# A graph layer over 1.65 million edges: 16 rows per block fetched one by one by SP and ACT beside POOL's gathers

## The chip, the core and the metric

The kernel runs on one core of one Trainium2 chip. The engines named here are PE (TensorE, matrix products), PEld (its weight loads), DVE (VectorE), ACT (ScalarE), POOL (GpSimd) and SP (SyncE, which issues transfers). The metric is the device time of one launch in microseconds (us). Before the change it was 15710.4 us, the median of three runs from 15699.01 to 15711.42 us.

## The reference

One layer of a graph network on 50000 nodes with 128 features each, followed by a residual and a normalization of each row. Every edge has a source node, a destination node and a type, 0 or 1, and the type chooses which of two weight matrices makes the message. The edges are sorted by destination.

```python
Xs = X[src]
m_data = Xs @ W_data.T + b_data
m_ctrl = Xs @ W_control.T + b_control
msg = jnp.where((edge_types == 0)[:, None], m_data, m_ctrl)
agg = jax.ops.segment_sum(msg, dst, num_segments=X.shape[0])
out = jax.nn.relu(agg + (X @ W_self.T + b_self))
x = _layernorm(x + out, axis=-1)
```

There are 1,650,000 edges: 800,000 random ones in both directions, and one loop from each node to itself.

## The kernel before, in words

The kernel doesn't compute a message per edge. It first sums the rows `x[src]` of all edges with the same destination and type, and multiplies these sums by the two weight matrices afterwards. The number of edges per destination and type is counted too, since each adds one bias.

The sorted edge list is cut into blocks. A block (`b`) has two steps (`Q = 2`), and a step has twelve chunks (`R = 12`) of 128 edges. For each chunk POOL issues one indirect DMA (L428, in `gathers`), which fetches 128 rows of 512 bytes, one to each partition. A pass is six chunks into one tile `y`; there are ten such tiles (`SLOTS = 10`), so POOL may be 60 gathers ahead of PE. A semaphore per tile says when the rows have landed, and PE waits for it at L435. Each step covers a window of 60 destinations (`W = 60`), and for each chunk PE multiplies the rows by a one-hot matrix `oh` (128 edges by 60 destinations by two types) into the sum `acc` of the step (L447). Two more small products add the counts (L451).

Loops from a node to itself need no fetched row, because the block's own rows of `x` are loaded anyway. Their places in the chunks are filled with other edges, up to `F = 42` per step (`fill`), so that a step takes 1536 + 42 edges from the list. The first block and the last one are plain: no places are filled there, and the last takes what is left over. With 3156 edges in a full block there are 523 blocks, 53 groups of ten, and the last block has 21 gathers.

DVE does most of the other work. Per block and in this order, it adds the last step's sum of the block before into a ring of three tiles (`add`, L458), begins the next tile (`begin_sums`, L471), makes the one-hot matrix two blocks ahead (`onehot`, L403) and its counts (`counts`, L411), fills the lists five blocks ahead (`fill`, L304 to L326, with an integer shift at L318), adds the first step's sum (L458), takes moments of the block before (L487 to L494) and makes a matrix `z` of the places that were filled (`left_out_matrix`, L341), which PE and then DVE (L358) use. Every second block it normalizes two blocks of rows (`store`, L509 and L512), after a square root on ACT (L503). Once in ten blocks it prepares the lists of the next group (`columns`, L212 to L282). Some of its operands are copied to PSUM first, `num_ps` and `lists` for instance.

PE's `layer(b - 1)` (L477 to L481) multiplies the sums by the weights; it stands in PE's order in block `b`, after the first two passes. SP loads the block's own rows three blocks ahead (`window`, L397), the edge lists of a group (`load_edges`, L159 and L161), the filling lists (L289 and L294) and stores the result (L517). ACT has only the square root to do in the steady state.

The order of the work is written out by hand (`tc.manual_schedule()`): each engine takes its instructions in the order of the program, and the loop over blocks at the end of `straight` sets that order. Semaphores between engines are placed by the framework, save those of the gathers.

Of the kernel before, what the change touches and what calls it, by code (L numbers as in the profile page):

```python
# [2 lines left out]

# [20 lines left out]
D = 128  # L24
ROW = 4 * D
# [8 lines left out]
R = 12  # L34
W = 60
Q = 2
PASS = 6
B = 112
C = R * Q
F = 42  # L40
R1 = R + 1
C1 = Q * R1
SIZES = [P] * R
SIZE = sum(SIZES)
CE = Q * SIZE
BE = CE + Q * F
NBLK = 2 + (E - CE) // BE
REST = E - CE - (NBLK - 2) * BE
REST_ROWS = [min(n, max(0, REST - q * SIZE - sum(SIZES[:r]))) for q in range(Q) for r, n in enumerate(SIZES)]
# [2 lines left out]
GB = 10  # L52
GROUPS = -(-NBLK // GB)
GC = GB * C1
AHEAD = 2
# [17 lines left out]
TBL = GROUPS * GB  # L73
# [4 lines left out]
def plain(b):  # L78

    return b == 0 or b >= NBLK - 1  # L80
# [3 lines left out]
    return bass.AP(tensor=ap.tensor, offset=ap.offset, ap=[[0, n], *ap.ap])  # L84


def straight(ctx, tc, c, x, x_t, edges_t, edges_f, dst_first, first_p, out):

# [12 lines left out]
    nc = tc.nc  # L101
# [3 lines left out]
    eds = ctx.enter_context(tc.tile_pool(name="eds", bufs=2))  # L105
# [48 lines left out]
    nc.vector.memset(stats, 0.0)  # L154
    loops = keep.tile([P, GROUPS], F32, name="loops")

    def load_edges(g):
# [219 lines left out]


    idxs = {0: idx0}
    bys, pcs, zs, pls, bases = {}, {}, {}, {}, {}  # L380
    ohs, cnts, accs, xTs, pos, hs, mvs, sds, os_ = {}, {}, {}, {}, {}, {}, {}, {}, {}

    BASES = 4
# [23 lines left out]
    def counts(b):  # L407

        cnt = ohp.tile([P, Q, 2 * W], BF16, name="cnt")
        with nc.allow_low_precision(reason="whole numbers up to R1"):  # L410
            nc.vector.tensor_reduce(cnt, ohs[b].rearrange("p (q r) w -> p q w r", r=R1), AX.X, ALU.add)  # L411
        cnts[b] = cnt

    landed = [tc.alloc_semaphore(f"landed{i}") for i in range(SLOTS)]
    seen = [0] * SLOTS
    pass_no = [0]
# [20 lines left out]
    def products(b, q, ks):  # L439
        y = gathers(b, ks)  # L440
        of_step = chunks_of(b, q)
        if ks[0] == of_step[0]:
            accs[b, q] = ps.tile([P, 3, W], F32, name="acc")
        acc = accs[b, q]
        for k in ks:
            r = REST_ROWS[k] if b == NBLK - 1 else SIZES[k % R]
            nc.tensor.matmul(acc[:, :2, :].rearrange("p t w -> p (t w)"), y[:r, k % PASS, :], ohs[b][:r, column(k), :],  # L447
                             start=k == of_step[0], stop=k == of_step[-1])
        if ks[-1] == of_step[-1]:
            for t in range(2):  # L450
                nc.tensor.matmul(acc[:, 2, :], to_row[:, t, :], cnts[b][:, q, t * W:(t + 1) * W],  # L451
                                 start=t == 0, stop=t == 1)
# [44 lines left out]
    def pair(b):  # L497

        return range(b // 2 * 2, b + 1) if b % 2 == 1 or b == NBLK - 1 else ()
# [19 lines left out]
    def find_bad():  # L519
# [35 lines left out]
    for b in range(1, RAHEAD):  # L555
        fill(b)
        left_out_columns(b)
        left_out_matrix(b)
        if b < AHEAD:
            onehot(b)  # L560
            counts(b)
        if b == 1:
            clear_sums()
    for b in range(NBLK + 1):
        if b == NBLK - 1:
            find_bad()
        if b + 3 < NBLK:
            window(b + 3)
        g, i = divmod(b, GB)
        if i == 0 and g + 1 < GROUPS:  # L570
            load_edges(g + 1)
        if i == 3 and g + 1 < GROUPS:
            spread_out(g + 1)
        if i == 4 and g + 1 < GROUPS:
            spread_in(g + 1)
        if b > 0:
            add(b - 1, steps_of(b - 1)[-1])
        if b < NBLK:
            begin_sums(b)
        if b + AHEAD < NBLK:  # L580
            onehot(b + AHEAD)
            counts(b + AHEAD)
        last = steps_of(b)[-1:]
        for q, (step, ks) in enumerate(passes_of(b)):
            if ks:
                products(b, step, ks)
            if q == 0 and b > 0:
                left_out_columns(b + RAHEAD - 1)
            if q == 0 and b + RAHEAD < NBLK:
                fill(b + RAHEAD)  # L590
            if q == 1 and b > 0:
                layer(b - 1)
            if q == 1:
                left_out_numbers(b + 1)
            if ks and step not in last and ks[-1] == chunks_of(b, step)[-1]:
                add(b, step)
            if q == 1 and b > 0:
                moments(b - 1)
# [235 lines left out]
@with_exitstack  # L834
def gnn_resnorm(
    ctx: ExitStack,
    tc: tile.TileContext,
    x: bass.AP,
    x_t: bass.AP,
    edges_t: bass.AP,  # L840
    edges_f: bass.AP,
    dst_first: bass.AP,
    first_p: bass.AP,
    src: bass.AP,
    dst: bass.AP,
    etype: bass.AP,
    w_data: bass.AP,
    b_data: bass.AP,
    w_ctrl: bass.AP,
    b_ctrl: bass.AP,  # L850
    w_self: bass.AP,
    b_self: bass.AP,
    out: bass.AP,
):

    nc = tc.nc  # L860
    const = ctx.enter_context(tc.tile_pool(name="const", bufs=1))

    ident = const.tile([P, P], F32, name="ident")
    make_identity(nc, ident)
    eps = const.tile([P, 1], F32, name="eps")
    nc.vector.memset(eps, EPS)
    wmsgT = const.tile([P, 2 * D], F32, name="wmsgT")
    wselfT = const.tile([P, D], F32, name="wselfT")
    w_all = const.tile([P, 3, D], F32, name="w_all")
    with tc.tile_pool(name="wts_ps", bufs=3, space=bass.MemoryType.PSUM) as wts_ps:  # L870
        for i, (w, o) in enumerate(((w_data, wmsgT[:, :D]), (w_ctrl, wmsgT[:, D:]), (w_self, wselfT))):
            w_sb = w_all[:, i, :]
            nc.scalar.dma_start(w_sb, w)
            pw = wts_ps.tile([P, D], F32, name="pw")
            nc.tensor.transpose(pw, w_sb, ident)
            nc.scalar.copy(o, pw)
    bad = const.tile([1, 1], I32, name="bad")
    c = dict(ident=ident, eps=eps, wmsgT=wmsgT, wselfT=wselfT, bad=bad,
             b_data=b_data, b_ctrl=b_ctrl, b_self=b_self)

    with ExitStack() as own:
        straight(own, tc, c, x, x_t, edges_t, edges_f, dst_first, first_p, out)
# [53 lines left out]
```

## Time and profile before

| what | value |
|---|---|
| median of the runs | 15710.4 us (15699.01 to 15711.42) |
| the profiled execution's own time | 15700.48 us |
| its span | 15698.7 us |
| granted TensorE clock | 0.53 of full speed |
| DMA packets | 563631, 935.70 MB, 60 GB/s |
| gathers by POOL | 12528 with lists from DVE and from the first load, 21 of the last block |

The profile is one execution of the program. Its page has the busy time of each engine, the span in 40 slices, the DMA queues, the chain of work that ended last, and groups of instructions. A group's line gives the line of the kernel, the engine, the operation, what it writes and reads with the shapes, its count, then its busy time in us and the mean ns of one, and then the idle time of the engine just ahead of these instructions with what ended it. "issue" is time in which an engine waited for nothing that the profile shows. Lines of the waits read: who waited, for what, in total us, how often, the longest. Lines of the timeline read: start in us, length in us, engine, line, operation, operands, count, and in brackets the idle time ahead with what ended it. PE's ends are modelled, and instructions follow one another in a pipeline, so the distance between starts tells more than lengths.

### The profile page before, as it was taken

What the parts mean: (1) busy time and instruction counts of PE and PEld (TensorE: products, weight loads), DVE (VectorE), ACT (ScalarE), POOL (GpSimd) and SP (SyncE); (2) the same over time, 40 slices, a digit from 0 to 9 for tenths busy, and PEclk for the clock granted to TensorE, in tenths of its full rate; (3) what the DMA queues carried; (4) which work ended last, traced back from release to release, by engine and by line L of the source; (5) the groups of instructions that cost most, each with busy time, mean ns of one, the idle gap of its engine ahead of it and who ended that gap; (6) DMA issues with size and microseconds to landing.
All of it is one profiled execution on the core that took longest, in us unless ns stands there. A gap on an engine that the chain in (4) does not pass through costs nothing. (4 is left out here: it accounts for less than half of the span.)

```text
span 15698.7 us, 108076 instructions
## 1 busy us (share of the span) xinstructions
PE 7588.4 (48%) x34677; PEld 6800.0 (43%) x34678; DVE 11054.2 (70%) x13586; ACT 80.8 (1%) x268; POOL 11852.3 (75%) x12559
## 2 busy tenths in 40 slices
PE   4444444444444444444444444444444444444444
PEld 3444444444444444444444444444444444444444
DVE  8766777777776776777777776677777777667775
ACT  0000000000000000000000000000000000000000
POOL 7777777777777777777777777777777777777777
PEclk6555555555555555555555555555555555555555
DMA  2222222222222222222222222222222222222222
GB/s 63 60 59 60 60 59 60 60 59 60 59 60 60 59 60 59 60 60 59 60 60 59 60 60 59 60 59 60 59 60 60 59 60 60 59 60 60 59 60 56
DMA packets 563631, 935.70 MB, mean 60 GB/s; under 512 B 289617, under 2 KB 348580, under 8 KB 563056
## 3 DMA queue, kind: packets, MB, share of 16 engines
q0 software_dynamic: 401600, 823.20, 20.2%
q1 hardware_dynamic: 161018, 105.30, 2.5%
q8 instruction: 281, 4.60, 0.1%
q14 instruction: 294, 2.41, 0.1%
q10 hardware_dynamic: 438, 0.20, 0.0%
HBM read 897.64 MB, written 30.17 MB: 59 GB/s over the span
## 5 line engine op out<-in xcount | busy, mean ns | idle before, releaser
L428 POOL DMA_INDIRECT y<-in_x,idx x12528 | 11830.7, 944 | 3824.1 <-issue 3568.3
L447 PE MATMUL acc<-oh,y 128*128 128x120 f32 x25098 | 6060.6, 431 | 7948.3 <-PEq L435 7948.3
L447 PEld LDWEIGHTS acc<-oh,y 128*128 128x128 f32 x25098 | 5478.4, 328 | 8434.5 <-PEq L435 8424.3
L458 DVE TENSOR_TENSOR sums<-acc,sums 128x180 f32 x1046 | 354.7, 339 | 4258.6 <-PE acc L451 4256.9
L411 DVE TENSOR_REDUCE cnt<-oh 128x240 bf16<-128x3120 f32 x523 | 3045.1, 5822 | 17.8
L403 DVE TENSOR_TENSOR oh<-col,small 128x3120 f32<-128x3120 f32 x523 | 1774.8, 3394 | 0.0
L326 DVE TENSOR_REDUCE by<-old 128x84 bf16<-128x1092 f32 x521 | 1108.0, 2127 | 18.1
L307 DVE TENSOR_TENSOR m<-rk,small 128x1092 f32<-128x1092 f32 x521 | 672.9, 1291 | 17.8
L310 DVE TENSOR_TENSOR new<-m,small 128x1092 f32<-128x1092 f32 x521 | 672.8, 1291 | 17.7
L314 DVE TENSOR_REDUCE v_new<-new 128x26 f32<-128x1092 f32 x521 | 672.5, 1291 | 17.7
L323 DVE TENSOR_TENSOR old<-m,small 128x1092 f32<-128x1092 f32 x521 | 668.8, 1284 | 0.0
L481 PE MATMUL po<-wmsgT,sums 128*112 128x128 f32 x2092 | 525.5, 394 | 0.0
L481 PEld LDWEIGHTS po<-wmsgT,sums 128*112 128x112 f32 x2092 | 381.6, 252 | 109.3 <-issue 87.5
L479 PE MATMUL po<-bias,sums 3*112 3x128 f32 x1046 | 355.6, 435 | 0.0
L451 PEld LDWEIGHTS <-to_row 128*128 128x128 bf16 x2092 | 328.7, 157 | 51.3
L471 DVE TENSOR_TENSOR sums<-pl,sums 128x336 f32<-128x336 f32 x521 | 264.4, 507 | 82.0 <-DVE sums L458 44.5
L451 PE MATMUL acc<-cnt,to_row 128*128 128x60 bf16 x2092 | 321.0, 247 | 0.0
L478 PE MATMUL po<-wselfT,xT 128*112 128x128 f32 x1046 | 319.9, 408 | 0.0
L478 PEld LDWEIGHTS po<-wselfT,xT 128*112 128x112 f32 x1046 | 281.7, 318 | 0.0
L479 PEld LDWEIGHTS po<-bias,sums 3*112 3x112 f32 x1046 | 209.6, 254 | 122.6 <-issue 113.9
L477 PE MATMUL po<-ident,xT 128*112 128x128 f32 x523 | 230.5, 441 | 0.0
L341 DVE TENSOR_SCALAR z<-node_no,at 84x256 bf16<-84x256 f32 x521 | 204.2, 392 | 18.4
(115 smaller groups left out, 3184.3 us busy)
## 6 DMA issues: line engine op xcount, KB each, us to landing
y<-in_x,idx POOLq DMA_INDIRECT x12528, 2.5
xT<-in_x_t SPq DMA_DIRECT2D x523, 56.0 KB, 1.9
out<-o SPq DMA_DIRECT2D x523, 56.0 KB, 1.6
vf_all<-vd SPq DMA_DIRECT2D x53, 420.0 KB, 3.6
sdt<-in_edges_t SPq DMA_DIRECT2D x53, 390.0 KB
sdt_f<-in_edges_f SPq DMA_DIRECT2D x53, 9.8 KB
vd<-v_f SPq DMA_DIRECT2D x53, 3.3 KB
first_i<-in_dst_first SPq DMA_DIRECT2D x1, 530.0 KB
```

Source lines behind the costliest of these rows:

```text
L307: nc.vector.tensor_tensor(m, rk_g[g][:, i, :, None].to_broadcast([P, C1, F]), rank_no_ps[:, None, :].to_broadcast([P, C1, F]), op=ALU.is_e ...
L310: nc.vector.tensor_tensor(new.rearrange("p (q r) f -> p q r f", r=R1), m.rearrange("p (q r) f -> p q r f", r=R1), vf.rearrange("p (q f) -> ...
L314: nc.vector.tensor_reduce(v, new, AX.X, ALU.add)
L323: nc.vector.tensor_tensor(old, m, cb[:, :, None].to_broadcast([P, C1, F]), op=ALU.mult)
L326: nc.vector.tensor_reduce(by, old.rearrange("p (q r) f -> p q f r", r=R1), AX.X, ALU.add)
L403: nc.vector.tensor_tensor(oh, col_g[g][:, i, :, None].to_broadcast([P, C1, 2 * W]), num_ps[:, None, :].to_broadcast([P, C1, 2 * W]), op=AL ...
L411: nc.vector.tensor_reduce(cnt, ohs[b].rearrange("p (q r) w -> p q w r", r=R1), AX.X, ALU.add)
L428: copy = nc.gpsimd.indirect_dma_start(out=y[:r, k % PASS, :].bitcast(U8), out_offset=None, in_=x_rows, in_offset=bass.IndirectOffsetOnAxis ...
L447: nc.tensor.matmul(acc[:, :2, :].rearrange("p t w -> p (t w)"), y[:r, k % PASS, :], ohs[b][:r, column(k), :], start=k == of_step[0], stop= ...
L451: nc.tensor.matmul(acc[:, 2, :], to_row[:, t, :], cnts[b][:, q, t * W:(t + 1) * W], start=t == 0, stop=t == 1)
L478: nc.tensor.matmul(po, xT, c["wselfT"], start=True, stop=False)
L481: nc.tensor.matmul(po, a[:, t, :B], c["wmsgT"][:, t * D:(t + 1) * D], start=False, stop=t == 1)
```

## The change

Each step takes eight more edges from the list, whose rows aren't gathered by POOL. SP and ACT fetch four of them each, with ordinary transfers of one row of 512 bytes. For that, the source numbers of these edges come in a list of their own (`src_x`), loaded on SP with the other lists of a group. DVE multiplies the 16 numbers of a block by the row size (`offsets`, three blocks ahead). SP and ACT each load eight of the results into registers with one instruction and issue eight transfers (`single_rows`, two blocks ahead, after the first pass of a block). PE waits for two semaphores once per block (`rows_fetched`) and adds one product with eight rows to each step's sum. The destination and type of these edges stand in the thirteenth column of the step's lists, which was there before and held no edges, so the one-hot matrix covers them without more work. A full block takes 3172 edges; there are 521 blocks, and the last one has 6 gathers.

```diff
+TURNS = (4, 4)
+S = sum(TURNS)
+LOADS = 1
+BEGIN = (0, -(-Q * TURNS[0] // 4) * 4)
+X = BEGIN[1] + -(-Q * TURNS[1] // 4) * 4
-BE = CE + Q * F
+BE = CE + Q * (F + S)
...
     def load_edges(g):
+        t = eds.tile([1, GB * X], I32, name="one_g")
+        nc.sync.dma_start(t, src_x[None, g * GB * X:(g + 1) * GB * X])
+        one_g[g] = t
...
+    ROW_SLOTS = AHEAD + 2
+    fetched = [[tc.alloc_semaphore(f"fetched{j}_{i}") for i in range(ROW_SLOTS)] for j in range(2)]
+
+    def offsets(b):
+        if not plain(b):
+            g, i = divmod(b, GB)
+            ats[b] = stp.tile([1, X], I32, name="at_x", bufs=AHEAD + 2)
+            nc.vector.tensor_scalar(ats[b], one_g[g][:, i * X:(i + 1) * X], float(ROW), None, op0=ALU.mult)
+
+    def single_rows(b, part):
+        if part == 0:
+            ys[b] = stp.tile([S, Q, D], F32, name="yx", bufs=ROW_SLOTS)
+        both = []
+        for j, (eng, dma) in enumerate(((SP, nc.sync), (ACT, nc.scalar))):
+            n = Q * TURNS[j]
+            k0, k1 = part_of(n, part), part_of(n, part + 1)
+            at = BEGIN[j]
+            _, rows = nc.values_load_multi_w_load_instructions(ats[b][0:1, at + k0:at + k1], engines=[eng], **RANGE)
+            both.append([(dma, fetched[j][b % ROW_SLOTS], *divmod(k0 + k, TURNS[j]), sum(TURNS[:j]), row)
+                         for k, row in enumerate(rows)])
+        for pair in zip_longest(*both):
+            for dma, sem, q, k, at, row in filter(None, pair):
+                copy = dma.dma_start(ys[b][at + k:at + k + 1, q, :].bitcast(U8), x_bytes[:, bass.ds(row, ROW)])
+                copy.then_inc(sem, 16)
...
+    def rows_fetched(b):
+        times = len(range(b % ROW_SLOTS or ROW_SLOTS, b + 1, ROW_SLOTS))
+        for j in range(2):
+            wait = nc.tensor.wait_ge(fetched[j][b % ROW_SLOTS], 16 * Q * TURNS[j] * times)
+        tc.declare_fence(wait.ins, group=f"single{b}")
...
         if ks[-1] == of_step[-1]:
+            if not plain(b):
+                if q == 0:
+                    rows_fetched(b)
+                nc.tensor.matmul(acc[:, :2, :].rearrange("p t w -> p (t w)"), ys[b][:, q, :],
+                                 ohs[b][:S, q * R1 + R, :], start=False, stop=True)
...
+    for b in range(1, AHEAD + 1):
+        offsets(b)
     columns(0)
...
             begin_sums(b)
+        offsets(b + AHEAD + 1)
         if b + AHEAD < NBLK:
             onehot(b + AHEAD)
...
+            if q < LOADS and not plain(b + AHEAD):
+                single_rows(b + AHEAD, q)
```

More of the change, by code (lines that the diff above doesn't have):

```diff
@@ L2 @@
 from contextlib import ExitStack
+from itertools import zip_longest
 import concourse.bacc as bacc
@@ L84, in row_bcast, with straight @@
     return bass.AP(tensor=ap.tensor, offset=ap.offset, ap=[[0, n], *ap.ap])
-def straight(ctx, tc, c, x, x_t, edges_t, edges_f, dst_first, first_p, out):
+def straight(ctx, tc, c, x, x_t, edges_t, edges_f, src_x, dst_first, first_p, out):
     nc = tc.nc
@@ L155, in straight @@
     loops = keep.tile([P, GROUPS], F32, name="loops")
+    one_g = {}
     def load_edges(g):
+        t = eds.tile([1, GB * X], I32, name="one_g")
+        nc.sync.dma_start(t, src_x[None, g * GB * X:(g + 1) * GB * X])
+        one_g[g] = t
         t = eds.tile([P, 3, GB, C1], I32, name="sdt", bufs=1)
@@ L379, in straight @@
     idxs = {0: idx0}
-    bys, pcs, zs, pls, bases = {}, {}, {}, {}, {}
+    bys, pcs, zs, pls, bases, ats, ys = {}, {}, {}, {}, {}, {}, {}
     ohs, cnts, accs, xTs, pos, hs, mvs, sds, os_ = {}, {}, {}, {}, {}, {}, {}, {}, {}
@@ L412, in counts, with part_of @@
         cnts[b] = cnt
+    ROW_SLOTS = AHEAD + 2
+    RANGE = dict(min_val=0, max_val=(N - 1) * ROW, skip_runtime_bounds_check_because="where a node's row is")
+    x_bytes = x.rearrange("n d -> (n d)").bitcast(U8)[None, :]
+    fetched = [[tc.alloc_semaphore(f"fetched{j}_{i}") for i in range(ROW_SLOTS)] for j in range(2)]
[4 more added lines that the diff above has]
+            nc.vector.tensor_scalar(ats[b], one_g[g][:, i * X:(i + 1) * X], float(ROW), None, op0=ALU.mult)
+    def part_of(n, part):
+        return min(n, 32 * part)
+    def single_rows(b, part):
[13 more added lines that the diff above has]
+                copy.then_inc(sem, 16)
+                tc.no_tile_sem_insts.add(copy.ins.name)
+                tc.add_to_no_dep_group(f"single{b}", copy.ins)
+    def rows_fetched(b):
[3 more added lines that the diff above has]
+        tc.declare_fence(wait.ins, group=f"single{b}")
     landed = [tc.alloc_semaphore(f"landed{i}") for i in range(SLOTS)]
@@ L447, in products @@
             nc.tensor.matmul(acc[:, :2, :].rearrange("p t w -> p (t w)"), y[:r, k % PASS, :], ohs[b][:r, column(k), :],
-                             start=k == of_step[0], stop=k == of_step[-1])
+                             start=k == of_step[0], stop=plain(b) and k == of_step[-1])
         if ks[-1] == of_step[-1]:
+            if not plain(b):
[3 more added lines that the diff above has]
+                                 ohs[b][:S, q * R1 + R, :], start=False, stop=True)
             for t in range(2):
@@ L561, in straight @@
             counts(b)
+            for part in range(LOADS):
+                single_rows(b, part)
         if b == 1:
@@ L841, in gnn_resnorm @@
     edges_f: bass.AP,
+    src_x: bass.AP,
     dst_first: bass.AP,
@@ L881, in gnn_resnorm @@
     with ExitStack() as own:
-        straight(own, tc, c, x, x_t, edges_t, edges_f, dst_first, first_p, out)
+        straight(own, tc, c, x, x_t, edges_t, edges_f, src_x, dst_first, first_p, out)
     found = nc.values_load(bad, min_val=0, max_val=4 * P,
@@ L904 @@
         rest = a[CE:].reshape(TBL - 1, BE)
-        steps = rest.reshape(TBL - 1, Q, SIZE + F)
+        steps = rest.reshape(TBL - 1, Q, SIZE + F + S)
         cols = np.full((TBL, Q, R1, P), pad, np.int32)
@@ L911 @@
             cols[NBLK - 1, :, r, :n] = rest[NBLK - 2, :CE].reshape(Q, SIZE)[:, at:at + n]
+        cols[1:NBLK - 1, :, R, :S] = steps[:NBLK - 2, :, SIZE + F:]
         fills = np.full((TBL, Q, F), pad, np.int32)
         fills[1:NBLK - 1] = steps[:NBLK - 2, :, SIZE:SIZE + F]
+        ones = np.full((TBL, X), pad, np.int32)
+        single = steps[:, :, SIZE + F:]
+        for j, n in enumerate(TURNS):
+            ones[1:, BEGIN[j]:BEGIN[j] + Q * n] = single[:, :, sum(TURNS[:j]):][:, :, :n].reshape(TBL - 1, Q * n)
         firsts = np.ascontiguousarray(cols[:, :, 0, 0])
@@ L916 @@
         fillers.append(fills.reshape(TBL * Q, F))
+        if k == "src":
+            arrays["src_x"] = ones.reshape(-1)
         if k == "dst":
@@ L929 @@
     with tile.TileContext(nc) as tc:
-        gnn_resnorm(tc, ap["x"], ap["x_t"], ap["edges_t"], ap["edges_f"], ap["dst_first"], ap["first_p"],
+        gnn_resnorm(tc, ap["x"], ap["x_t"], ap["edges_t"], ap["edges_f"], ap["src_x"], ap["dst_first"], ap["first_p"],
                     ap["src"], ap["dst"], ap["edge_type_2"],
```

## The prediction

> **What bounds the kernel now.** I read the page's busy table first, then its groups, then the waits of POOL, then the timeline of one block and of the end.
>
> ```profile
> span 15698.7 us, 108076 instructions
> PE 7588.4 (48%) x34677; PEld 6800.0 (43%) x34678; DVE 11054.2 (70%) x13586; ACT 80.8 (1%) x268; POOL 11852.3 (75%) x12559
> L428 POOL DMA_INDIRECT y<-in_x,idx x12528 | 11830.7, 944 | 3824.1 <-issue 3568.3
> L447 PE MATMUL acc<-oh,y 128*128 128x120 f32 x25098 | 6060.6, 431 | 7948.3 <-PEq L435 7948.3
> L458 DVE TENSOR_TENSOR sums<-acc,sums 128x180 f32 x1046 | 354.7, 339 | 4258.6 <-PE acc L451 4256.9
> ...
> POOL y L428 <- issue: 3574.7, 11728, 0.3
> POOL y L428 <- PE acc L447: 3.5, 2, 3.2
> POOL y L428 <- DVE idx L318: 2.1, 1, 2.1
> ```
>
> No engine is busy over 75%, yet one has no slack. A gather is 0.944 us of work and 0.305 us of POOL's own issue, and (11830.7 + 3824.1) / 12528 = 1.2496 us per gather accounts for nearly the whole span. Read gather by gather, the distance between starts is 1.244 to 1.260 us in 99 of 100. POOL waited for others only twice, both at the start; the idle times of 0.3 us that other lines put down to PE or DVE are the same issue time. PE and DVE sit idle waiting for rows: PE 7948 us for landed gathers, DVE 4257 us for PE's sums. So the time is the number of gathers times 1.2496 us, plus a start and an end. A block of 24 gathers lasts 30.0 us.
>
> **What goes.** A full block takes 2·(1536+42) = 3156 edges before, and 2·(1536+42+8) = 3172 after, with the same 24 gathers. Blocks: 2 + (1650000 − 3072)//3156 = 523, and 2 + 1646928//3172 = 521. Rest for the last block: 2652 edges in 21 gathers before, 660 in 6 after. Gathers: 522·24 + 21 = 12549 before, 520·24 + 6 = 12486 after. 63 fewer, by 1.2496 us: **−78.7 us**. All of it is on the path, if the pitch stays.
>
> **SP and ACT.** Each gets 519 blocks times one register load and 8 one-row transfers. The nearest rows are SP's window load (0.37 us to issue) and ACT's one-row bias loads (0.23 to 0.56 us): 8 × 0.37 + 0.3 = 3.3 us per queue in a 30 us block. They are issued in the order of block b, for block b+2, and PE needs them some 45 us later. On SP the next window load (three blocks ahead) and the stores queue behind them; on ACT a square root each second block, which only a normalization waits for. Cost 0 under this cover. Without it, a late row would stop PE, and POOL only after the 60 gathers (75 us) that its ten slots hold.
>
> **The DMA engines.** The gathers take 20.2% of them, all else 2.8%; 8304 transfers of 512 bytes add about 4 MB to 936. What they do to POOL's pitch the trace does not show directly. Nearest: gathers beside the 1046 window loads and stores stand within 1 ns of the others. Bounds −1 to +1 ns per transfer, ±8 us; I take 0.
>
> **PE.** One product more per step, two matmuls. In the block below, twelve loads run from 8014.52 to 8017.02, so a pair is 0.42 us; 1038 steps make 436 us beside 7948 us idle. Cost 0 for PE, but each step's sum is ready 0.42 us later.
>
> **DVE.** One small multiplication per block (L437 after: 1x16). Nearest rows: 0.14 us for 1x1 (L536), 0.18 us for 128x26 (L318); back to back such operations start 0.08 us apart. 519 × 0.08 = 42 us beside 4257 us idle: cost 0 for DVE's own time.
>
> **Where the two shifts matter.** DVE's chain of a block starts at the wait for the last step's sum and runs without another wait to z (L341). So z moves by 0.42 + 0.08 = 0.50 us against the gathers, whose beat stays. The timeline shows why that can cost:
>
> ```profile
> 8006.89 0.94 POOL L428 DMA_INDIRECT y<-in_x,idx  x1 [0.30 <-issue]
> 8007.54 0.41 DVE L341 TENSOR_SCALAR z<-node_no,at 84x256 bf16<-84x256 f32 x1
> 8008.14 0.94 POOL L428 DMA_INDIRECT y<-in_x,idx  x1 [0.30 <-issue]
> 8014.52 2.64 PEld L447 LDWEIGHTS acc<-oh,y 128*128 128x128 f32 x12 [4.87 <-PEq L435]
> 8017.02 0.36 PEld L451 LDWEIGHTS <-to_row 128*128 128x128 bf16 x2
> ...
> 11513.73 0.35 DVE L341 TENSOR_SCALAR z<-node_no,at 84x256 bf16<-84x256 f32 x1
> 11513.84 1.06 POOL L428 DMA_INDIRECT y<-in_x,idx  x1 [0.30 <-issue]
> ```
>
> Usually z starts 0.55 to 0.68 us after a gather and disturbs nothing (it is itself held, 0.41 for 0.35 us); in some 200 blocks at 0.92, because an integer shift ahead of it (L318) was held in the same way, which 0.5 us later it no longer is. In the last two lines DVE was late, z began 0.11 us ahead of a gather, and the gather took 1.06 for 0.94 us. Eight z of 521 did this: leads of 0.19, 0.15, 0.13 and 0.11 us cost 0.04, 0.07, 0.09 and 0.11 us, that is 0.22 minus the lead. Two that began 0.05 us after a gather's start cost nothing; between a lead of 0.10 and those there is no row. After the change z stands at 0.65 + 0.50 = 1.15 us, a lead of 0.10, with a spread of about ±0.06 from block to block. That is the edge. I take half the blocks at 0.10 us each: 519 × 0.05 = **+26 us**. Low end: all miss, 0. High end by the rows: all at 0.12 us, 62 us. The other ten-block work of DVE (L214, L267) prolongs some gathers today, about 8 us in all; it may vanish or double, ±8 us.
>
> A rule of the Trainium skill speaks against the change here ("SBUF — State Buffer", section "Who interferes with whom"): a tensor_scalar in a two-port mode and a GpSimd operation exclude each other for the whole instruction, whichever comes second waiting. By it each z and each new multiplication could hold a gather for its length, by an estimate from the rows 519 × (0.35 + 0.15) = 260 us, and the kernel would end near 15900 us. The rows above agree that either side can wait, but not that each overlap costs POOL.
>
> **Start and end.** The first index list and PE's first products hang on DVE's preparation (the waits of 2.1 and 3.2 us). One more load is issued on SP before first_i (0.4 us), and two multiplications come first: **+0.7 us**. At the end the last block has one pass instead of four, and the layer of the block before it no longer hides beside later gathers. PE's order puts it after the last rows, then DVE's moments and stores, and only then the last sum:
>
> ```profile
> 15686.95 0.44 PE L477 MATMUL po<-ident,xT 128*112 128x128 f32 x1
> 15687.17 0.35 DVE L458 TENSOR_TENSOR sums<-acc,sums 128x180 f32 x1 [6.48 <-PE acc L451]
> 15688.45 1.20 PE L481 MATMUL po<-wmsgT,sums 128*112 128x128 f32 x4
> 15689.68 0.29 DVE L487 COPY h<-po 112x128 f32<-112x128 f32 x1 [2.16 <-PE po L481]
> ```
>
> Added are a layer (15686.95 to 15689.65: 2.7 us), moments (1.2), root and reciprocal (0.5), two normalizations (0.6) and the add (0.5), less 0.3 to 0.5 us of the last layer that no longer waits: **+5 us** (3 to 6).
>
> **Sum.** −78.7 + 26 + 0.7 + 5 = −47 us, against the profiled execution's own 15700.5 us (span 15698.7 and 1.8 around it). That execution is 9.9 us below the median of the runs shown (15699.0 to 15711.4). On the median: 15710.4 − 47 = **15663 us**.
>
> **Rivals.**
> 1. z lands in front of every gather and each lead counts. Between leads of 0.10 and 0 there is no row; if the line 0.22 minus lead went on, 0.20 us per block would cost 104 us, and −78.7 + 5.7 + 104 = +31 us gives 15741 us, **slower** by 0.2%. It decides from 73/519 = 0.14 us per block on. For it: the line holds in all eight rows, and the shift points just there. Against it: two z 0.05 us after a start were harmless, and when z comes while POOL is using the port, z waits, as its 0.41 us show.
> 2. z misses every gather, because the shift is 0.60 rather than 0.50 us (a product more than 0.42 us, a multiplication waiting on its two queues). Then −73 us: 15637 us.
> 3. The one-row transfers drag on the gathers, or arrive late and stop PE. At 5 ns per gather the first costs 62 us: 15726 us. The 1 ns beside transfers of 56 KB speaks against it, and the 45 us of lead against the second; but ACT has issued no DMA in the steady state so far, so this is not seen.
> 4. The change does not do what it says: the count of gathers is fixed by the sizes and not by the chip, so only the pitch is open. I give this nothing.
>
> **How the numbers follow.** About 0.2% (31 us) is what can be told from no change. Forecast, collisions of 10 to 42 us: 0.50, at 15647 to 15679. Rival 2: 0.20, faster. Collisions of 42 to 104 us: 0.17, within 0.2%. Rival 1 beyond that: 0.08, slower. Rival 3: 0.05, of which 0.03 slower. Together faster 0.70, same 0.19, slower 0.11. The range runs from the case without collisions less the 12 us between runs, 15625, to collisions of 85 us, 15722; below lies about 0.04, above about 0.15. Cases of both signs are in it; the forecast's own range is 15640 to 15685.
>
> **What the profile after would show.** POOL's indirect group counts 12480 and 6. Its mean is 944 ns by rival 2, 946 by the forecast (26 us over 12486), 952 by rival 1, so single gathers beside z tell more. Right: z starts 0.0 to 0.2 us ahead of a gather, about half of those gathers at 1.04 to 1.06 us; idle per gather stays 0.305 us; no wait of PE on fetched rows; the last gather stands some 21 us before the end instead of 16.5. Wrong: a pitch that is longer in all gathers (rival 3), gathers of 1.1 us and more in each block (rival 1), or a POOL wait named after PE, DVE or a DMA in the steady state.

## The result and the profile after

The changed kernel takes 15660.9 us (median of eight runs, 15648.8 to 15663.2), the kernel before beside it 15711.4 us (eight runs, 15699.0 to 15711.8). The ratio is 0.9967, with a 95% interval of 0.9958 to 0.9976, so it is faster by 50 us. The forecast was 15663 us.

The page of the changed kernel, its first lines and the groups that answer to those shown of before, with the two groups of the new product:

```profile
span 15647.0 us, 131554 instructions
PE 8613.2 (55%) x36591; PEld 7366.1 (47%) x36592; DVE 10976.1 (70%) x14057; ACT 80.4 (1%) x267; POOL 11812.9 (75%) x12496
L483 POOL DMA_INDIRECT y<-in_x,idx x12480 | 11805.8, 946 | 3811.4 <-issue 3798.0
L502 PE MATMUL acc<-oh,y 128*128 128x120 f32 x24972 | 6041.8, 432 | 6881.0 <-PEq L490 6872.5
L508 PE MATMUL acc<-oh,yx 8*128 8x120 f32 x2076 | 806.8, 490 | 0.0
L508 PEld LDWEIGHTS acc<-oh,yx 8*128 8x128 f32 x2076 | 515.4, 307 | 218.7 <-issue 218.1
L518 DVE TENSOR_TENSOR sums<-acc,sums 128x180 f32 x1041 | 352.7, 339 | 4279.8 <-PE acc L511 4279.5
```

Its waits of POOL, as who waited, for what, total us, times, longest:

```profile
POOL y L483 <- issue: 3799.8, 12466, 0.3
POOL y L483 <- DVE idx L329: 3.9, 1, 3.9
POOL y L483 <- PE acc L502: 3.2, 1, 3.2
```

POOL bounds the kernel as before: it waits for others only at the start, and its gathers, 12480 and the 6 of the last block, stand 1.25 us apart. The idle time of PE for landed rows fell from 7948 to 6872 us; it does more and waits less. Two marks differ from before. A gather has a mean of 946 instead of 944 ns, and the wait for DVE's first list is 3.9 instead of 2.1 us.

The profiled execution took 15648.8 us, 12 us below the median, as that of before was 11 us below its own. Between the two traces the span fell by 51.8 us. Read gather by gather, it divides so (a gather is called prolonged where it took over 959 ns, and what it took beyond 944 ns is counted):

| term | before | after | difference, us |
|---|---|---|---|
| gathers, by 1.2496 us | 12549 | 12486 | −78.7 |
| prolonged gathers after the start | 7.7 us in 96 | 28.9 us in 207 | +21.2 |
| first gather with a list of DVE waits | 1.82 us | 3.55 us | +1.7 |
| start of the last gather to the end | 16.5 us | 21.1 us | +4.6 |
| rest | | | −0.6 |

Which operation of DVE ended a prolonged gather's delay can be read from the times: 26.4 us of the 28.9 lie beside three operations of `columns`, the preparation of the lists once in ten blocks (L226, L241, L280), 1.2 us beside z, which is L352 now, and some 1.0 us beside the normalization. The timeline of one such place in the changed kernel:

```profile
999.18 0.43 DVE L226 TENSOR_TENSOR col<-col,rel 128x260 f32<-128x260 f32 x1
999.26 1.17 POOL L483 DMA_INDIRECT y<-in_x,idx  x1 [0.30 <-issue]
...
1001.84 0.43 DVE L241 SCALAR_TENSOR_TENSOR v<-sdt,lim 128x260 f32<-128x260 int32 x1
1001.98 1.11 POOL L483 DMA_INDIRECT y<-in_x,idx  x1 [0.30 <-issue]
...
1003.28 0.43 DVE L280 TENSOR_TENSOR cb<-cb,base 128x260 f32<-128x260 f32 x1
1003.39 1.13 POOL L483 DMA_INDIRECT y<-in_x,idx  x1 [0.31 <-issue]
```

Each of the three starts 0.08 to 0.14 us ahead of a gather, and the gather takes 0.17 to 0.23 us longer. It repeats in 50 of the 53 groups. And this is z in a usual block, with the new product ahead of it:

```profile
8000.34 0.50 PEld L508 LDWEIGHTS acc<-oh,yx 8*128 8x128 f32 x2 [0.21 <-issue]
8000.34 0.78 PE L508 MATMUL acc<-oh,yx 8*128 8x120 f32 x2
8001.05 0.13 PEld L511 LDWEIGHTS <-to_row 128*128 128x128 bf16 x2 [0.21 <-issue]
...
8021.07 0.94 POOL L483 DMA_INDIRECT y<-in_x,idx  x1 [0.30 <-issue]
8021.35 0.35 DVE L352 TENSOR_SCALAR z<-node_no,at 84x256 bf16<-84x256 f32 x1
8022.32 0.94 POOL L483 DMA_INDIRECT y<-in_x,idx  x1 [0.30 <-issue]
```

z starts 0.28 us after a gather, neither is prolonged, and so it is in 449 of 519 blocks (0.2 to 0.5 us after a start). The first three lines say why z is so late: ahead of the eight-row weights, and again behind them, the weight loads stand idle for 0.21 us without waiting for anything.

### The profile page after: what moved, and what is told of

Its sections match the earlier page's. It is cut to its first block, busy times and chain, and to the rows that moved or that the text cites. A ratio compares the mean times of both kernels' runs of the same rounds, so it can differ in the third digit from the quotient of the medians.

```text
span 15647.0 us, 131554 instructions
## 1 busy us (share of the span) xinstructions
PE 8613.2 (55%) x36591; PEld 7366.1 (47%) x36592; DVE 10976.1 (70%) x14057; ACT 80.4 (1%) x267; POOL 11812.9 (75%) x12496
## 4 chain that ended last, share of the span: by engine, by line
POOL 73%; issue 24%; DVE 2%; PE 0%; POOLq 0%; DMA 0%; DVEq 0%; PEldq 0%; ACT 0%; ACTq 0%
POOL y L483 73%; DVE cnt L422 1%; DVE oh L414 0%; POOLq L483 0%; PE acc L502 0%; DMA y<-in_x,idx 0%; DVE m L318 0%; DVE new L321 0%; DVE v_new L325 0%; DVE old L334 0%; DVE by L337 0%; PE acc L508 0%; DVE sums L518 0%; DMA first_i<-in_dst_first 0%; DVE at_x L437 0%
## 5 line engine op out<-in xcount | busy, mean ns | idle before, releaser
L508 PE MATMUL acc<-oh,yx 8*128 8x120 f32 x2076 | 806.8, 490 | 0.0
L541 PE MATMUL po<-wmsgT,sums 128*112 128x128 f32 x2084 | 623.1, 455 | 0.0
L508 PEld LDWEIGHTS acc<-oh,yx 8*128 8x128 f32 x2076 | 515.4, 307 | 218.7 <-issue 218.1
L541 PEld LDWEIGHTS po<-wmsgT,sums 128*112 128x112 f32 x2084 | 456.4, 299 | 129.6 <-issue 129.6
L539 PE MATMUL po<-bias,sums 3*112 3x128 f32 x1042 | 398.2, 484 | 1.1 <-DVE sums L518 1.1
L511 PEld LDWEIGHTS <-to_row 128*128 128x128 bf16 x2082 | 133.4, 107 | 218.6 <-issue 218.0
```

Of the source, the lines that this page charges most:

```text
L539: nc.tensor.matmul(po, a[0:3, 2, :B], bias, start=False, stop=False)
L541: nc.tensor.matmul(po, a[:, t, :B], c["wmsgT"][:, t * D:(t + 1) * D], start=False, stop=t == 1)
```

## The experiments

The experiments ran on four chips, called A to D here. On A and B the kernel before took 15696 to 15697 us, and on C and D 17847 to 17848 us. Each ratio is against the kernel before on the same chip. The kernel before and the changed one, whose traces are compared above, ran on another chip, of the kind of A and B, where the kernel before took 15711 us. The times that the first expectations name count from that chip, so it is the gains that compare; and where the changed kernel's 50 us stand beside a gain on chip A, the two come from different chips.

### Only fewer gathers

```diff
-        t = eds.tile([1, GB * X], I32, name="one_g")
-        nc.sync.dma_start(t, src_x[None, g * GB * X:(g + 1) * GB * X])
...
-                             start=k == of_step[0], stop=plain(b) and k == of_step[-1])
+                             start=k == of_step[0], stop=k == of_step[-1])
...
-                nc.tensor.matmul(acc[:, :2, :].rearrange("p t w -> p (t w)"), ys[b][:, q, :],
-                                 ohs[b][:S, q * R1 + R, :], start=False, stop=True)
...
-        offsets(b + AHEAD + 1)
...
-                single_rows(b + AHEAD, q)
```

> The 16 edges per block that SP and ACT fetch are left out of the sums altogether: no one-row transfers, no registers, no products with eight rows, no multiplication of offsets, no list of them. The gathers are 12486 as in the changed kernel. Theory (time is gathers times 1.2496 us plus start, end and collisions of DVE with gathers): DVE stands where it stood before, so collisions stay at 8 us; -78.7 us for 63 gathers, +4.6 us for the longer end, no longer start: -74 us against the kernel before, about 15637 us. Rival (the missing 28 us of the 79 lie in the pitch or the end and not in what was added): about -50 us, 15661 us.

Measured on chip A: 15623.3 us against 15696.2, ratio 0.9953 (0.9937 to 0.9970), 73 us less. Its largest group:

```profile
span 15622.6 us, 107583 instructions
L480 POOL DMA_INDIRECT y<-in_x,idx x12480 | 11781.6, 944 | 3809.9 <-issue 3552.8
```

The mean is back at 944 ns. Prolonged gathers come to 3.7 us, and the last gather stands 22.5 us before the end. So 63 gathers fewer are worth about what was worked out: 78.7 us, less 5.9 for the longer end, and 4.0 more because fewer gathers are prolonged, make 76.8, and from trace to trace the span fell by 76.1. All that the change adds costs some 23 us (73 − 50).

### The products without the transfers

```diff
-                if q == 0:
-                    rows_fetched(b)
-                nc.tensor.matmul(acc[:, :2, :].rearrange("p t w -> p (t w)"), ys[b][:, q, :],
+                nc.tensor.matmul(acc[:, :2, :].rearrange("p t w -> p (t w)"), blank[:, q, :],
                                  ohs[b][:S, q * R1 + R, :], start=False, stop=True)
...
+    blank = keep.tile([S, Q, D], F32, name="blank")
+    nc.vector.memset(blank, 0.0)
...
-                single_rows(b + AHEAD, q)
```

> The changed kernel without the 16 one-row transfers, their register loads and PE's wait for them; the products with eight rows stay and read a tile that was cleared once, so these edges are missing from the sums. Theory: the transfers cost POOL nothing and DVE's place against the gathers is kept by the product, so the time is that of the changed kernel, 15661 us within 6 us. Rival (transfers on the hardware queues drag on POOL's gathers): some 20 us less, 15640 us.

Measured on chip A: 15648.3 us against 15696.2, ratio 0.9969 (0.9958 to 0.9981), 48 us less.

```profile
span 15646.6 us, 112360 instructions
L483 POOL DMA_INDIRECT y<-in_x,idx x12480 | 11805.7, 946 | 3810.6 <-issue 3796.8
```

Without any of the 8304 transfers POOL's group is that of the changed kernel to 0.1 us of busy time, with 29.1 us in prolonged gathers, most of them beside the same three operations. The transfers cost POOL nothing.

### The transfers without the products

```diff
-            if not plain(b):
-                if q == 0:
-                    rows_fetched(b)
-                nc.tensor.matmul(acc[:, :2, :].rearrange("p t w -> p (t w)"), ys[b][:, q, :],
-                                 ohs[b][:S, q * R1 + R, :], start=False, stop=True)
+            if not plain(b) and q == 0:
+                rows_fetched(b)
```

> The changed kernel without the product with eight rows; the rows are fetched and waited for, and their edges are missing from the sums. Theory: each step's sum is ready 0.85 us earlier, DVE stands within 0.1 us of where it stood before the change, and its ten-block work prolongs gathers by about 8 us instead of 29: 15640 us. Rival (the prolonged gathers come from the transfers): 15661 us.

Measured on chip A: 15627.9 us against 15696.2, ratio 0.9956 (0.9940 to 0.9973), 68 us less. Prolonged gathers come to 7.6 us in 90. At the place in the trace where the changed kernel loses three times, this one stands so:

```profile
996.39 0.43 DVE L226 TENSOR_TENSOR col<-col,rel 128x260 f32<-128x260 f32 x1
997.27 0.94 POOL L483 DMA_INDIRECT y<-in_x,idx  x1 [0.31 <-issue]
...
999.12 0.43 DVE L241 SCALAR_TENSOR_TENSOR v<-sdt,lim 128x260 f32<-128x260 int32 x1
...
999.77 1.12 POOL L483 DMA_INDIRECT y<-in_x,idx  x1 [0.30 <-issue]
999.79 0.28 DVE L278 TENSOR_SCALAR cb<-sdt 128x260 f32<-128x260 int32 x1
...
1000.56 0.43 DVE L280 TENSOR_TENSOR cb<-cb,base 128x260 f32<-128x260 f32 x1
1001.19 0.94 POOL L483 DMA_INDIRECT y<-in_x,idx  x1 [0.30 <-issue]
```

The same three operations start 0.63 to 0.88 us ahead of the next gather, and cost nothing; what is left beside L278 was there before the change too. So of the 23 us that the additions cost, some 18 come with the product (68 − 50; on chip A alone, 68 − 48 = 20 between this kernel and the one with the products only), and not because PE has more to do, but because the sum of each step, and with it DVE's work, comes later. The multiplication and the transfers have the other 5 at most (73 − 68). The same kernel on chip B:

> The fetched rows are not multiplied into the sums, so their edges are missing from the result; all else is as in the changed kernel. On a chip where PE bounds the kernel (there the change cost 41 us in both sets of runs), theory: the added product is what costs there, as PE does in each of 521 blocks two products more; without it PE's work per block is that of before and there are two blocks fewer, so the time is 521/523 of the kernel before's, 0.4% or some 68 us below it. Rival: the transfers of SP and ACT cost there, and without the product the time stays 0.2% above the kernel before. On a chip where POOL bounds it: 68 us below the kernel before, as measured.

It took 15628.2 us against 15696.9 there, ratio 0.9956 (0.9940 to 0.9973), the same 69 us. POOL bounds the kernel on that chip too, so what the product costs on a chip like C, which the expectation asks, is not known.

### The product with 128 rows

The rows that no transfer fills are cleared once, so their part of the product is zero.

```diff
+    rows_at = [keep.tile([P, Q, D], F32, name=f"yx{i}") for i in range(ROW_SLOTS)]
+    for t in rows_at:
+        nc.vector.memset(t, 0.0)
...
-            ys[b] = stp.tile([S, Q, D], F32, name="yx", bufs=ROW_SLOTS)
+            ys[b] = rows_at[b % ROW_SLOTS]
...
-                                 ohs[b][:S, q * R1 + R, :], start=False, stop=True)
+                                 ohs[b][:, q * R1 + R, :], start=False, stop=True)
```

> The changed kernel with the product over 128 rows, of which 120 are zero and cleared once, instead of eight: the same result. Theory: PE no longer empties between shapes, the product takes 0.43 instead of 0.85 us, and DVE moves to where the forecast had put it, z about 0.1 us ahead of a gather. Gathers beside z then take 0.05 to 0.12 us longer in about half of the blocks, +26 us, and the ten-block work has another place too (0 to 26 us): 15650 to 15690 us, 15670 in the middle, with some 250 gathers over 0.97 us of which most stand beside z. Rival (z never prolongs a gather, whatever its place): not over 15661 us, with no more such gathers beside z than in the changed kernel, 14.

Measured on chip A: 15660.7 us against 15696.2, ratio 0.9977 (0.9968 to 0.9987), 35 us less. The group of the product's weight loads, and then z in one block from the timeline:

```profile
L511 PEld LDWEIGHTS acc<-oh,yx 128*128 128x128 f32 x2076 | 565.7, 332 | 0.0
```

```profile
7396.06 0.35 DVE L352 TENSOR_SCALAR z<-node_no,at 84x256 bf16<-84x256 f32 x1
7396.20 1.03 POOL L486 DMA_INDIRECT y<-in_x,idx  x1 [0.30 <-issue]
7397.53 0.94 POOL L486 DMA_INDIRECT y<-in_x,idx  x1 [0.30 <-issue]
```

There is no idle time ahead of the weights. From the last gathered chunk's weight load to that of the counts it is 0.197 us before the change (median of all steps, as in the kernel with fewer gathers only), 0.623 us here, and 1.253 us in the changed kernel. The product adds 0.43 us with 128 rows, just the 0.42 of the forecast, and 1.06 us with eight (the expectations took 0.85). The granted clock was 0.508 in the changed kernel and 0.555 here, but that is not the reason: on chip C, below, the changed kernel had 0.555 as well and its 1.252 us were the same. With 0.43 us, what the forecast described came about: z stands 0.10 to 0.20 us ahead of a gather in 304 of 519 blocks, and z alone prolongs 321 gathers by 22.3 us (26 were forecast). Where the lead was 0.10 to 0.15 us the mean cost was 0.094 us, and at 0.15 to 0.20 us 0.053 us. In 71 blocks z was less than 0.05 us ahead, and there the cost was nil (0.5 ns). So the line "0.22 minus the lead" holds down to 0.10 us and does not go on to zero.

This kernel's product ends sooner, and yet by the two gains the kernel is 15 us slower than the changed one (13 us slower than the kernel without the transfers, on the same chip), because of where z falls: its prolonged gathers come to 39.5 us in all. The three `columns` operations of the changed kernel cost it almost nothing (0.7 us in all), while others of the same chain, L223, L225 and L278, cost 16.0.

### A delay of the ten-block work, and more rows

DVE clears a tile of 128x300 ahead of `columns`, which moves the ten-block operations:

```diff
+    idle = keep.tile([P, 300], F32, name="idle")
...
+                nc.vector.memset(idle, 0.0)
                 columns(g + 1)
```

More rows take only sizes: sixteen by each of SP and ACT per step, or 32, loaded in two parts.

```diff
-TURNS = (4, 4)
+TURNS = (16, 16)
```

```diff
-TURNS = (4, 4)
+TURNS = (32, 32)
-LOADS = 1
+LOADS = 2
```

> The changed kernel once more, beside the three others of this chip. Expected by every theory: 45 to 55 us below the kernel before, some 29 us of prolonged gathers, nearly all of them beside the operations that prepare the lists once in ten blocks.

> One more operation for DVE, once in ten blocks: it clears a tile of 128x300 ahead of the preparation of the lists, by an estimate from the 0.35 us of an operation on 84x256 some 0.3 us. Theory (what is left of the collisions is a matter of where the ten-block operations start against the gathers, and 0.3 us later their starts no longer lie just ahead of a gather): prolonged gathers fall from about 29 us to 5 to 10 us, and the time lies some 20 us below the changed kernel's, although DVE does more. Rival A (the operations hold POOL wherever they lie, because each reads two operands or is long): prolonged gathers stay at 25 to 33 us and the time stays within 5 us of the changed kernel's. Rival B (later operations in the same chain move onto the gathers in place of the first ones): prolonged gathers rise above 33 us, the time rises by as much.

> Four times as many single rows: 16 per step by each of SP and ACT, so 32 rows per step and 513 blocks, with 12300 gathers instead of 12486. Theory (a row fetched by SP or ACT costs POOL nothing as long as each queue issues its 32 transfers in a block's 30 us; at 0.33 us each they take some 10.6 us): 186 gathers fewer by 1.2496 us, 232 us less than the changed kernel, some 15420 to 15440 us; the collisions may change by 20 us either way, since the larger multiplication and product shift DVE's work again. Rival (the transfers drag on the gathers once they are many: 1 ns per transfer beside a gather would be 32800 transfers by 1 ns = 33 us, 5 ns 164 us): the pitch of all gathers grows beyond 1.2496 us and the gain stays below 200 us. Rival (SP's window load and stores come late behind the transfers): a wait on the window load appears in PE or DVE and POOL waits on a slot.

> Eight times as many single rows: 32 per step by each of SP and ACT, 64 rows per step, 503 blocks and 12061 gathers, the registers loaded in two parts per block. Theory: 425 gathers fewer than the changed kernel by 1.2496 us, 531 us less, some 15120 us, if each queue gets its 64 transfers (by 0.33 us, 21 us) and its other work into a block of 30 us. Rival (queues are now nearly full, and the block's own rows, the stores and the square root wait behind the transfers): PE waits for fetched rows or DVE for the square root, POOL for its slots, and the time falls by less than 400 us or rises.

All four ran on chip C, where the kernel before took 17846.6 us. There the changed kernel is slower: 17889.0 us, ratio 1.0024 (1.0015 to 1.0034). The delay gave 17890.8 us (1.0025, 1.0015 to 1.0035), sixteen rows each 18085.9 us (1.0133, 1.0116 to 1.0150), and 32 rows each 23842.9 us (1.3357, 1.3334 to 1.3379). Every expectation missed, since each had POOL as the bound. Of the changed kernel on chip C, the page's chain of work that ended last, by engine, then waits, and then the timeline around one stall:

```profile
DVE 40%; another core or an unknown queue 29%; issue 17%; PE 13%; DVEq 1%; SPq 0%; DMA 0%; ACT 0%; ACTq 0%
```

```profile
PEld acc L502 <- issue: 6176.5, 3143, 23.5
POOL y L483 <- issue: 3592.1, 11775, 0.5
DVE sums L518 <- remote: 3011.2, 423, 21.6
POOL y L483 <- remote: 1793.4, 490, 4.8
...
POOL y L483 <- PE acc L502: 271.4, 67, 4.8
```

```profile
8016.49 0.36 PE L502 MATMUL acc<-oh,y 128*128 128x120 f32 x1 [1.33 <-issue]
8019.29 0.36 PE L502 MATMUL acc<-oh,y 128*128 128x120 f32 x1 [2.44 <-issue]
...
8025.86 0.95 POOL L483 DMA_INDIRECT y<-in_x,idx  x1 [3.44 <-remote]
```

PE's products, which need nothing but the rows that had landed, stand 2.8 us apart here instead of 0.21, with a weight load midway, so one instruction every 1.40 us; in other stretches it is 0.70. There are some 470 such stretches in 521 blocks, a typical one 15 to 17 us long. In the changed kernel's first trace and in the kernel with 128 rows on chip A there is none. The single rows of SP and ACT show the same steps on C, eight in 11.3 us in one block where they took 2.6 on the first chip.

POOL, which never waits in the steady state on the other chips, waits there in 490 places that the profile can't name, for up to 4.8 us. They lie at the border of a pass of six gathers, where the code has the wait for a free tile, and in some 180 more places, 625 us in all, the profile names PE as what ended the wait; so I read them as PE being later than the ten tiles allow. Together POOL's waits take 2208 us beyond its own issue time, nearly all of the 2235 us by which the span is longer than on the first chip. The chain that ended last, 73% POOL on the first chip, has no share of POOL here: it runs over DVE, waits without a name, issue and PE. So it is shown that POOL alone no longer sets the time there, but not that PE does; and which of PE, SP and ACT, all of which got work, makes the change lose is open.

The granted clock does not explain it, for it is no lower there (0.555 against 0.508 for the changed kernel, 0.598 against 0.530 for the kernel before), nor do the DMA packets: those of 4 KB took 221 ns, as in the kernel with 128 rows on chip A (220), and 243 in the changed kernel's first trace. What slows the instruction streams on these chips stays open, and also how the 42 us divide between the product and the transfers there (there is no trace of the kernel before on such a chip). With 32 rows each the rival's wait came about as well: PE's weight loads wait 15079 us for fetched rows, 495 times, while SP and ACT, in one place, issue 55 transfers in some 40 us. Where POOL is the bound that kernel has not been tried.

The delay and sixteen rows each also ran on chip D:

> The delay of the ten-block operations once more, for the last chip was one where PE was the bound (its instructions stood 0.7 or 1.4 us apart in stretches, POOL waited for slots, and the kernel before took 17847 us). If POOL bounds the kernel again, theory: the time lies 15 to 25 us below the changed kernel's, so 60 to 75 us below the kernel before on the same chip, and prolonged gathers fall from 29 us to 5 to 10 us. Rival A: prolonged gathers stay at 25 to 33 us, the time 47 to 50 us below the kernel before. Rival B: other operations of the chain move onto the gathers, the gain over the kernel before falls below 40 us. If PE bounds it again, the time is that of the changed kernel there, 0.2 to 0.3% above the kernel before.

> Four times as many single rows, once more. If POOL bounds the kernel, theory (a row fetched by SP or ACT costs POOL nothing while its queue has the time; 32 transfers by 0.33 us are 10.6 us of a block's 30 us): 249 gathers fewer than before by 1.2496 us, less some 30 us for the end, the start and collisions, so 270 to 300 us below the kernel before on the same chip. Rival (the transfers drag on the gathers): less than 240 us. Rival (a queue of SP or ACT is too full, as on the last chip, where transfers stood 0.9 to 1.4 us apart): PE waits for fetched rows, and the time is above the kernel before's. If PE bounds it, the time is 1 to 1.5% above the kernel before, as on the last chip.

Chip D behaves as C: 17889.6 us with the delay (1.0023, 1.0013 to 1.0033) and 18098.1 us with sixteen rows each (1.0139, 1.0122 to 1.0156). The delay has thus not been tried where POOL is the bound.

Sixteen rows each also ran on chip A:

> Four times as many single rows, on a chip where POOL bounds the kernel, if it is one. Theory (a row fetched by SP or ACT costs POOL nothing while its queue has the time; 32 transfers by 0.33 us are 10.6 us of a block's 30 us): 249 gathers fewer than before by 1.2496 us, 311 us; less 30 us for the start, the end and collisions, so 270 to 300 us below the kernel before, some 15400 to 15425 us. Rival (the transfers drag on the gathers, 1 to 5 ns for each of 32704): a pitch above 1.2496 us between all gathers, and a gain below 240 us. Rival (queues too full): PE waits for fetched rows and POOL for slots, and the gain is lost.

There it takes 15418.2 us against 15696.8, ratio 0.9823 (0.9806 to 0.9839): 279 us less than before, where the changed kernel gained 50. The page, and SP's and ACT's transfers from the timeline:

```profile
span 15416.6 us, 178612 instructions
L483 POOL DMA_INDIRECT y<-in_x,idx x12288 | 11625.4, 946 | 3754.2 <-issue 3741.8
L508 PEld LDWEIGHTS acc<-oh,yx 32*128 32x128 f32 x2044 | 507.4, 307 | 215.3 <-issue 214.7
```

```profile
8025.20 7.04 ACTq L457 DMA_DIRECT2D yx<-in_x  x20
8028.78 3.33 SPq L457 DMA_DIRECT2D yx<-in_x  x9
```

The 32704 transfers, 0.32 us apart on their queues, hardly touch POOL's pitch: the idle time per gather is still 0.305 us (without the few long waits 305.0 ns on average for 304.8 before, which makes 3 us in 12300 gathers), and the mean 946 ns is that of the changed kernel, with 28.5 us in prolonged gathers, 24.1 of it beside the same operations of `columns`. Fewer gathers are worth 311.2 us, of which prolonged gathers take 20.8, the longer end 4.4 and the start 0.5 back. That would be 285.5 us. From trace to trace the span fell by 282.1, short by the 3 us of idle time; the rest of the way to 279 is that the trace of before is from the first chip, where it took 15700.5 us against 15696.8 on chip A. Between the weight loads it is 1.253 us as with eight rows: so four times as many rows, 32 in place of eight, cost PE no more per step. Not every load under 128 rows pays this: one with 20 rows, in the last block of the changed kernel, has 0.2 us of idle time ahead of it, and those with 92 rows (the last block before) and 100 (the last block here) have none.

## Why the prediction was right

The total was right, 50 us gained with 47 forecast, but part of that is luck: two of its terms were wrong, z by 25 us too much and the ten-block work by 20 us too little, and they made up for each other.

- **POOL sets the time, and fewer gathers count in full:** right. The kernel with nothing but fewer gathers gained 73 us, where −78.7 and +5 had been worked out; part of the agreement there is 4.0 us of prolonged gathers that it no longer has.
- **SP, ACT and the DMA engines at no cost:** right. The bound of ±8 us was wide; without the transfers the gain is 48 us on chip A, with them 50 on the first chip. In the block read, eight transfers took 2.6 and 2.7 us on the two queues where 3.0 were estimated, and the register load ahead of them 0.7 where 0.3 were: together the 3.3 of the forecast. The waits of the changed kernel show none of PE for fetched rows. Rival 3 falls, on the chips where POOL is the bound.
- **PE, "a pair is 0.42 us":** this is the step that failed. The price came from loads with 128 rows and was used for loads with eight. It measured 1.06 us. The page of before had a nearer row, the three-row bias product in the layer:

```profile
L479 PEld LDWEIGHTS po<-bias,sums 3*112 3x112 f32 x1046 | 209.6, 254 | 122.6 <-issue 113.9 <-DVE sums L458 1.2
```

  Its idle time is put down to "issue"; 128-row loads that follow one another have none. The Trainium skill states that the rows of the weights don't matter for the time of a load, only its columns ("TensorE: Matmul & The Clock Gate", section "Step-by-step: what each phase is for"). For the load alone that agrees, a mean of 307 ns with eight rows and 332 with 128. That section says nothing of the idle time on both sides, 0.42 us together, which makes up most of the 0.63 us that the product costs beyond the forecast. PE has the time, so nothing is lost on PE itself; but each step's sum comes 1.06 us later and not 0.42.
- **z, +26 us:** z cost 1.2 us. With so large a shift it passes the gather and starts behind it. With the 0.42 us that were assumed, the term is right: 22.3 us in the kernel with 128 rows.
- **The ten-block work, "±8 us":** mis-sized. It is +20 us (26.5 after, 6.6 before), and the same shift is the reason, since without the product it is gone. The text reckoned with the operations that touched gathers before (L214 and L267 there), and not with the others of the same chain, which were harmless only by their place. Each touch of theirs costs 0.17 to 0.23 us and three follow one another.
- **The start, +0.7, and the end, +5:** +1.7 and +4.6 us.

Rival 2 had the right mechanism, a shift over 0.60 us, and the wrong price: it took z alone and gave 15637 us. Rival 1 rested on a line that goes on to a lead of zero; 71 blocks at leads under 0.05 us in the kernel with 128 rows, and 19 in the changed one, show no cost. Of the signs that were named, the mean of 946 ns, the idle time of 0.305 us and the last gather 21 us before the end came about. z ahead of a gather, and gathers of 1.04 us beside it in half the blocks, did not.

The Trainium skill's rule that a tensor_scalar in a two-port mode and a GpSimd operation exclude each other for the whole instruction ("SBUF — State Buffer", section "Who interferes with whom") would by the forecast's estimate have put the kernel near 15900 us. The profile doesn't tell in which mode z ran. In this trace most of the 519 z lie wholly within a gather and prolong it by nothing; what counts is where the operation starts against the gather.

What the forecast did not see at all is that it holds for one kind of chip. On chip C the same change costs 0.2%, and on D, where only variants of it ran, the one with the delay does.

## What to carry to other kernels

Price a small operation by the row with its own shape: eight weight rows in place of 128 made the product longer, 1.06 us for 0.43. An edit that costs nothing on an idle engine still moves what waits for it, and when that work meets a periodic engine the cost is set by where all of it falls, so look at each operation of the moved chain and not only at those that collide now. A row fetched by an idle queue is a cheap way to relieve a gathering engine, but only while that engine is the bound: measure on more than one chip before taking it.

## What was not expected of the hardware

- Between weight loads of 128 rows and of 8 or 32 (f32) the loading stands idle 0.21 us, on the way in and on the way out. A product of two such loads makes the step 1.06 us longer, with 128 rows 0.43 us. Loads with 92 and 100 rows showed no such idle time.
- An operation of DVE ahead of a gather delays it by 0.22 us minus the lead, for z of 0.35 us and leads of 0.10 to 0.20 us; with under 0.05 us there is no delay. No z in 519 blocks of the kernel with 128 rows stands at 0.05 to 0.10. The place that costs is not the same for all operations: L278 in the kernel without the products started 0.02 us behind a gather and still made it 0.18 us longer.
- The four chips of the experiments are of two kinds. On two of them, C and D, stretches occur in which instructions of PE, SP and ACT start 0.70 or 1.40 us apart without a wait that the trace shows, and the kernel before takes 17847 instead of 15696 us.
